# Attention scores from split queries and keys: one float32r product over 64 rows, and a second product for the maxima

## The chip, the cores and the metric

The kernel runs on one core of a Trainium2 chip. The metric is the device time of one execution in microseconds, the median of repeated runs. The core has a matrix engine (PE, with its weight loads PEld), three vector-like engines (DVE, ACT, POOL), SyncE (SP), whose queue issues every DMA of this kernel, and 16 DMA engines that share the transfers.

## The reference

A decoder layer on 32 samples of 256 tokens and 256 channels, with layer normalization after each of three blocks: a selective-scan block, cross attention with 16 heads of 16 channels, and eight gated experts, each for 32 of the 256 tokens of a sample.

```python
def reference(x, ctx, ...):
    x = layernorm(x + scan_block(x))            # xr = x W_in; conv; silu; dA, dBu; 4 chunks of 64 steps
    x = layernorm(x + cross_attention(x, ctx))
    x = layernorm(x + experts(x))               # silu(x w1) * (x w3), then w2

def cross_attention(query, ctx):                # 16 heads, d_k = 16
    q, k, v = proj(query, w_q, b_q), proj(ctx, w_k, b_k), proj(ctx, w_v, b_v)
    scores = einsum('bhqd,bhkd->bhqk', q, k) / sqrt(16)
    out = einsum('bhqk,bhkd->bhqd', softmax(scores), v)
    return einsum('bsd,ed->bse', merge_heads(out), w_o) + b_o
```

## The kernel before

**Order of the work.** The kernel is written as some 24 chains (Python generators, listed from L1255 on). Each chain yields the time at which its next step may begin and the engine of that step; `in_order` (L80) picks the earliest, with lags as tie breakers, and lets it emit its instructions. `spend` (L54) adds a planned cost to an engine's clock; the costs are constants in the text (`MM` 0.47 us a matmul, `GP` for POOL, `ISSUE` 0.62 and `LANDING` 3.5 for a DMA). The result is one fixed program order for each engine, SP included. At run time semaphores hold each engine at the head of its own order.

**Scan.** A sample has 16 steps of 32 channels. For a step, two loads (`load_step`, L519) copy delta and delta times u from DRAM (`dd`) into 128 partitions, eight copies of each channel pair; their source is [16, 8, 512] with a repeat in the middle. Loads are issued three steps ahead. ACT makes four exponentials (L573), DVE a product (L602) and the scan (L621), POOL multiplies by C (L637), PE sums (L651) and frees the six `h` buffers.

**Attention.** `keys_ahead` (L691) projects keys and values of a sample and stores them to DRAM (`k_all`, `v_all`); `queries` (L789) projects the queries from the normalized first block and stores them to `heads`. `spread_heads` (L678) loads both back so that 16 heads lie in 8 groups of two: head h is group h // 2, and its 16 channels begin at partition 64 (h % 2). `kT` and `qT` have 64 rows for each of two heads, of which rows 16 to 62 stay zero. A sample is worked in two halves of 8 heads, each loaded on its own; sample b's half waits until `attns` has scored that half of sample b - 1.

`maxima` (L825) computes the scores of two heads at a time, queries as weights, over 63 rows; DVE takes the row maxima (L838), PE transposes them, ACT negates them (L847), and two DMAs carry them through DRAM (`tops`) into row 63 of `qT`. Row 63 of `kT` is one (L272 to L275). `attns` (L874) then computes the scores again with keys as weights over all 64 rows, so that each score arrives with its row's maximum subtracted; ACT exponentiates (L894) and PE multiplies by the values (L863). `finish` (L924) normalizes, applies `w_o` and stores to `x2d`.

**Experts.** 32 units work on 256 tokens of one expert from eight samples, or, for the last eight samples, 128 tokens of each of two experts from four. A unit's tokens are read from `x2d` by `rows_of` (L1065), a block of [4, 32, 256] for each of two transfers, and results are stored in the same form to `out`. They fill PE time at low rank; the last four units can only begin when the last sample is stored.

**Shared parts.** Five PSUM banks go round through `take` and `done`. `heads(n)` (L166) loads the projection weights and biases for q and k, from an array padded to 32 columns for each head; these loads are put off into `later` and issued by `rest` (L363). `product` (L343) and `biased` (L352) are the helpers for a projection and its evacuation.

Of the kernel before, what the change touches and what calls it, by code (L numbers as in the profile page):

```python
# [7 lines left out]

F32 = mybir.dt.float32
AF = mybir.ActivationFunctionType  # L10
ALU = mybir.AluOpType
AX = mybir.AxisListType
# [3 lines left out]
P = 128  # L16
B, L, D = 32, 256, 256
# [14 lines left out]
H, DK = 16, 16  # L32
NG = 4
HG, HR = 8, 64
# [5 lines left out]
LANDING = 3.5  # L40
# [5 lines left out]
class Clock:  # L46
# [7 lines left out]
    def spend(self, engine, us, after=0.0):  # L54

        self.at[engine] = max(self.at[engine], after, self.base) + us
        return self.at[engine] + 0.3
# [40 lines left out]
def decoder_kernel(ctx: ExitStack, tc: tile.TileContext, a: dict, out: bass.AP):  # L98
    nc = tc.nc
    clock = Clock()  # L100
    spend = clock.spend

    def dma(dst, src):

        nc.sync.dma_start(dst, src)
        spend("SP", ISSUE)
# [4 lines left out]
    ident = cpool.tile([P, P], F32, name="ident")  # L111
# [3 lines left out]

    x2d = dram.tile([B, L, D], F32, name="x2d")

    k_all = dram.tile([B, D, L], F32, name="k_all")
    v_all = dram.tile([B, L, D], F32, name="v_all")

    ph = ctx
# [41 lines left out]
        dma(t, a[name].partition_broadcast(P))  # L163
        return t

    def heads(n):  # L166

        w = wp.tile([P, 2, D], F32, tag="w_" + n, name="w_" + n)
        src = a["w_" + n].rearrange("(k p) (h c) -> p k h c", p=P, c=32)
        for k in range(2):  # L170
            dst = w[:, k].rearrange("p (h c) -> p h c", c=DK)
            dma(dst, src[:, k, :, :DK])
        bias = wp.tile([P, 2], F32, name="b_" + n)
        for g in range(NG):
            r = 64 * (g % 2)
            src = a["b_" + n].rearrange("(j c) g -> j c g", c=32)[:, :DK, g : g + 1]
            dma(bias[r : r + 64, g // 2 : g // 2 + 1], src)
        return w, bias


# [25 lines left out]
            dma(at, src[j, g].unsqueeze(1).to_broadcast([DL, NL, NDC * NS]))  # L206
    nc.scalar.preload_act_table_set("natural_log_exp_and_others")

    later = []
    now, dma = dma, lambda dst, src: later.append((dst, src))  # L210
    w_k, b_k = heads("k")
    w_v = weight("w_v", D, D)
    b_out = row("b_out")
    w_out = weight("w_out", DI, D)
    w_q, b_q = heads("q")
    w_o = weight("w_o", D, D)
    b_o = row("b_o")
    b_v = wp.tile([P, 2, 1], F32, name="b_v")
# [49 lines left out]
    nc.gpsimd.memset(v[:, :, :, DK : DK + 1], 1.0)  # L268


    kT = keep.tile([P, HG, L], F32, name="kT")
    last = small.tile([P, 1], F32, tag="ln_st", name="last")  # L272
    at = ident.rearrange("p (j c) -> p j c", c=HR)[:, :, HR - 1]
    nc.vector.tensor_reduce(last, at, AX.X, ALU.add)
    nc.vector.tensor_copy(kT.rearrange("p g t -> p (g t)"), last.to_broadcast([P, HG * L]))  # L275
    qT = keep.tile([P, HG, L], F32, name="qT")
    nc.gpsimd.memset(qT, 0.0)

    tops = [keep.tile([P, 2, 4, 2], F32, name=f"tops_{i}") for i in range(2)]

# [82 lines left out]

    def rest():

        while later:
            yield 0.0, "SP"
            dma(*later.pop(0))

    xps, dds, sress, bcds, ygs, us, spread, silus = {}, {}, {}, {}, {}, {}, {}, []  # L370
    gated, stored = {}, []
# [303 lines left out]
    kts, qts, tts, vts, x1Ts, attended, oSs, ending = {}, {}, {}, {}, {}, [], [], []  # L675
    scored = {}

    def spread_heads(b, dst, d, t, there):  # L678

        yield t, "SP"  # L680
        for half in range(2):
            if b:
                yield lambda: max(t, scored[b - 1, half]) if (b - 1, half) in scored else None, "SP"
            for j in range(2):
                src = d.rearrange("(i g j c) t -> i j c g t", i=2, j=2, c=DK)[half, j]
                dma(dst[HR * j : HR * j + DK, 4 * half : 4 * half + 4, :], src)
            there[b, half] = clock.at["SP"] + LANDING

    made = []
# [1 line left out]
    def keys_ahead():  # L691

        for b in range(B):
            rank = lambda: 2 if b < len(begun) + 1 else 3
            yield lambda: None if later else spread.get(0), "SP"
            load_ctx(b)
            t0 = clock.at["SP"] + 2 * LANDING
            ctxT = cts.pop(b)
            yield from take(1, rank, t0)
            ps, t = product(  # L700
                "ps_qk",
                lambda j: [w_k[:, k, j * P : (j + 1) * P] for k in range(2)],
                lambda j: [ctxT[:, k, :] for k in range(2)],
            )
            yield t, "ACT"
            flat = unit1.tile([P, 2, L], F32, tag="k_flat", name=f"k_flat_{b}")
            tk = biased(flat, AF.Identity, b_k, ps, 0)
            done(1, tk)
            yield tk, "SP"
            dma(k_all[b].rearrange("(m p) t -> p m t", p=P), flat)  # L710
            yield from take(1, rank, t0)
            ps, t = product(
                "ps_v",
                lambda t: [ctxT[:, k, t * P : (t + 1) * P] for k in range(2)],
                lambda t: [w_v[:, k, :] for k in range(2)],
            )
            yield max(t, clock.at["SP"] + LANDING), "ACT"
            flat = unit1.tile([P, 2, D], F32, tag="k_flat", name=f"v_flat_{b}")
            nc.scalar.copy(flat, ps)
            t = spend("ACT", EV[2])  # L720
            done(1, t)
            yield t, "SP"
            dma(v_all[b].rearrange("(t p) c -> p t c", p=P), flat)
            made.append(clock.at["SP"] + LANDING)
# [64 lines left out]
    def queries():  # L789
        for b in range(B):  # L790
            yield lambda: x1Ts[b][1] if b in x1Ts else None, "PE"
            x1T, tx = x1Ts[b]
            yield from take(1, 2, tx)
            ps, t = product(
                "ps_qk",
                lambda j: [w_q[:, k, j * P : (j + 1) * P] for k in range(2)],
                lambda j: [x1T[:, k, :] for k in range(2)],
            )
            yield t, "ACT"
            del x1Ts[b]  # L800
            flat = unit1.tile([P, 2, L], F32, tag="q_flat", name=f"q_flat_{b}")
            tq = biased(flat, AF.Identity, b_q, ps, 0)
            done(1, tq)
            yield tq, "SP"
            d = bcd.tile([D, L], F32, tag="heads", name="heads")
            dma(d.rearrange("(m p) t -> p m t", p=P), flat)
            yield from spread_heads(b, qT, d, clock.at["SP"] + LANDING, qts)

    def scores(heads, left, right, n):


        ss = [bank("s").rearrange("p (t n) -> p t n", t=2) for _ in heads]
        for t in range(2):
            for h, s in zip(heads, ss):
                g, r = h // 2, HR * (h % 2)
                nc.tensor.matmul(  # L816
                    s[:, t, :],
                    left[r : r + n, g, t * P : (t + 1) * P],
                    right[r : r + n, g, :],
                    start=True,  # L820
                    stop=True,
                )
        return ss, spend("PE", 2 * MM + 0.2)

    def maxima():  # L825

        for i in range(2 * B):
            b, half = i // 2, i % 2
            at = b, half
            yield lambda: max(qts[at], kts[at]) if at in qts and at in kts else None, "PE"  # L830
            top, t0 = tops[half], max(qts[at], kts[at])
            h = 0
            while h < 8:
                yield from take(2, 2, t0)
                ss, ts = scores(range(8 * half + h, 8 * half + h + 2), qT, kT, HR - 1)
                for s in ss:
                    yield ts, "DVE"
                    nc.vector.tensor_reduce(top[:, h % 2, h // 2, :], s, AX.X, ALU.max)  # L838
                    t = spend("DVE", VE[2])
                    done(1, t)  # L840
                    h += 1
            yield from take(1, 1, t)
            ps = bank("ps_m")[:H, :P]
            nc.tensor.transpose(ps, top.rearrange("p j g t -> p (j g t)"), ident)
            yield spend("PE", 0.2), "ACT"
            rows = unit2.tile([H, P], F32, tag="rows", name="rows")
            nc.scalar.activation(rows, ps, AF.Identity, scale=-1.0)  # L847
            t = spend("ACT", 0.35)
            done(1, t)
            yield t, "SP"  # L850
            d = bcd.tile([2, 4 * L], F32, tag="tops", name="tops")
            dma(d.rearrange("j (i n) -> (j i) n", n=P), rows)
            yield clock.at["SP"] + LANDING, "SP"
            dst = qT[HR - 1 :: HR, 4 * half : 4 * half + 4]
            dma(dst.rearrange("j g t -> j (g t)"), d)
            tts[b, half] = clock.at["SP"] + LANDING

    def attend(g, ess):
# [15 lines left out]
    def attns():  # L874

        for n in range(2 * B):
# [4 lines left out]
            for g in range(3):  # L881
                ess = []
                while g < 2 and len(ess) < 4:
                    yield from take(2, 2, tq)
                    h = 8 * half + 4 * g + len(ess)
                    ss, ts = scores(range(h, h + 2), kT, qT, HR)
                    if g and not ess:
                        yield lambda: vts.get(b), "PE"
                        yield from take(1, 3, max(te, vts[b]))
# [34 lines left out]
    def finish(b):  # L924
# [25 lines left out]
        yield from take(1, 3, t)  # L950
        ps, t = transposes(att.rearrange("p t h d -> p t (h d)"))
        yield t, "ACT"
        aT = unit1.tile([P, 2, L], F32, tag="aT", name=f"aT_{b}")
        nc.scalar.copy(aT, ps)
        t = spend("ACT", EV[2])
        done(1, t)
# [385 lines left out]
```

## Time and profile before

| | us |
|---|---|
| runs | 2745.47, 2744.92, 2738.03; median 2744.92 |
| the profiled execution | 2743.78 |
| its span, first to last instruction | 2742.0 |
| first L621 scan starts | 44 |
| last L621 scan ends | 2513 |
| PE busy on score products (two L816 rows) | 345.4 + 313.8 |
| DVE busy on scans L621, products L602, maxima L838 | 1168.9, 626.1, 325.2 |
| POOL busy on L637 | 1209.1 |
| DMA | 505.86 MB in 491,497 packets |

A line of the profile names the source line, the engine, the operation, the tiles it writes and reads, shapes and the number of instructions; after the bar stand the busy time of the group in us and the mean ns of one, then the engine's idle time before them and what ended it. One f32 product of the program appears as two PE records. A DMA shows the landing of its parts in the updates of its semaphore, which the trace holds with their times. "Samples" below are the 32 entries of the batch.

### The profile page before, as it was taken

The page shows a single profiled execution, that of the slowest core. Times are in us where ns is not written, and L with a number is a line of the kernel's source. Part 1 is how long each engine was busy: PE and PEld are TensorE (multiplying, and loading weights), DVE is VectorE, ACT ScalarE, POOL GpSimd, SP SyncE. Part 2 cuts the span into 40 slices and gives each one's busy share as a digit, 9 for nine tenths or more (in the row PEclk, how much of TensorE's full clock was granted, in tenths as well). Part 3 has the DMA queues.
Part 4 walks back from the last instruction along what each step waited for, and adds up shares of the span by engine and source line. Part 5 has one row for each costly group of instructions (what it writes and reads, how often), then busy time and mean ns, then how long its engine had stood idle before and what let it go on. Part 6 is the DMA issues. An engine that isn't in the chain of part 4 may idle for free.

```text
span 2742.0 us, 48659 instructions
## 1 busy us (share of the span) xinstructions
PE 2466.3 (90%) x16964; PEld 1705.3 (62%) x16964; DVE 2380.6 (87%) x2413; ACT 2043.4 (75%) x4327; POOL 1643.7 (60%) x1145
## 2 busy tenths in 40 slices
PE   5788989889899899989998989999999899998988
PEld 4565666566566666666666666665666566666767
DVE  4999999999999999999999999999999899896212
ACT  6887888888778878887878778888788788674331
POOL 4775766666666666575666665666666666553000
PEclk8899999999999999998999999999999999999999
DMA  7866666666676666676666666667666566666464
GB/s 203 228 199 176 193 187 181 189 191 191 187 199 186 181 167 190 176 197 177 167 198 187 198 175 186 187 177 195 190 197 179 163 172 180 185 174 181 150 195 144
DMA packets 491497, 505.86 MB, mean 184 GB/s; under 512 B 177204, under 2 KB 339252, under 8 KB 491252
## 3 DMA queue, kind: packets, MB, share of 16 engines
q1 hardware_dynamic: 491252, 502.75, 64.8%
q8 instruction: 135, 2.21, 0.4%
q14 instruction: 110, 0.90, 0.1%
HBM read 426.07 MB, written 76.55 MB: 183 GB/s over the span
## 4 chain that ended last, share of the span: by engine, by line
PE 29%; DVE 11%; ACT 8%; DMA 5%; issue 3%; POOL 1%; SPq 1%; DVEq 0%; ACTq 0%; POOLq 0%
PE ps_h L1133 8%; PE s L816 6%; DVE h L621 5%; PE ps_down L1212 4%; ACT da L573 3%; PE y L651 3%; DVE bu L602 2%; DVE tops L838 2%; PE ps_in L349 2%; PE ps_oT L863 2%; DMA ld<-dd 1%; DMA xe<-x2d 1%; PE ps_out L349 1%; PE ps_qk L349 1%; ACT es L894 1%
## 5 line engine op out<-in xcount | busy, mean ns | idle before, releaser
L637 POOL TENSOR_TENSOR h<-h,c_bc 128x1024 f32<-128x1024 f32 x512 | 1209.1, 2362 | 740.6 <-DVE h L621 627.0
L621 DVE TENSOR_TENSOR_SCAN h<-da,bu 128x1024 f32<-128x1024 f32 x512 | 1168.9, 2283 | 50.4 <-ACT da L573 5.8
L573 ACT ACTIVATE da<-ld,a_neg 128x252 f32<-128x252 f32 x2048 | 864.6, 504 | 188.3 <-DVE h L621 138.4
L602 DVE TENSOR_TENSOR bu<-ld,b_bc 128x1024 f32<-128x1024 f32 x512 | 626.1, 1223 | 19.9 <-DMA ld<-dd 8.0
L816 PE MATMUL s<-kT,qT 63*128 63x256 f32 x2048 | 345.4, 416 | 45.6 <-DVE tops L838 22.8
L894 ACT ACTIVATE es<-s 128x512 f32<-128x512 f32 x512 | 277.9, 594 | 140.6 <-PE s L816 75.9
L838 DVE TENSOR_REDUCE tops<-s 128x2 f32<-128x512 f32 x512 | 325.2, 677 | 41.6 <-PE s L816 41.1
L1133 PE MATMUL ps_h<-x2T,w 128*128 128x256 f32 (+2 forms) x1536 | 343.5, 368 | 9.5 <-ACT es L894 1.7
L816 PE MATMUL s<-qT,kT 64*128 64x256 f32 x2048 | 313.8, 405 | 22.5 <-DMA qT<-tops 13.0
L651 PE MATMUL y<-h,sel_y 128*32 128x256 f32 x4096 | 280.8, 397 | 52.3 <-POOL h L637 36.9
L816 PEld LDWEIGHTS s<-kT,qT 63*128 63x128 f32 x2048 | 213.8, 193 | 151.9 <-DVE tops L838 50.8
L1133 PEld LDWEIGHTS ps_h<-x2T,w 128*128 128x128 f32 (+1 forms) x1536 | 246.7, 186 | 89.7 <-issue 35.1
L349 PE MATMUL ps_in<-xT,w_in 128*128 128x256 f32 x1024 | 258.4, 397 | 8.7 <-ACT da L573 2.6
L816 PEld LDWEIGHTS s<-qT,kT 64*128 64x128 f32 x2048 | 200.9, 189 | 102.3 <-issue 39.6
L651 PEld LDWEIGHTS y<-h,sel_y 128*32 128x32 f32 x4096 | 131.8, 113 | 177.4 <-POOL h L637 55.1
L349 PEld LDWEIGHTS ps_in<-xT,w_in 128*128 128x128 f32 x1024 | 192.8, 196 | 60.4 <-issue 12.9
L420 POOL TENSOR_TENSOR u<-u,shifted 128x512 f32<-128x512 f32 x128 | 151.4, 1183 | 39.7 <-ACT u L407 34.7
L323 POOL TENSOR_SCALAR ln_rstd<-ln_mv 128x2 f32<-128x2 f32 x96 | 20.9, 218 | 254.2 <-DVE ln_mv L320 250.0
L407 ACT ACTIVATE shifted<-ps_in,tap_b,conv_w 128x256 f32<-128x256 f32 x256 | 130.8, 567 | 22.5 <-PE ps_in L349 10.9
L863 PE MATMUL ps_oT<-es,v 128*32 128x256 f32 x2048 | 142.4, 391 | 3.7 <-DVE h L1197 1.2
L349 PE MATMUL ps_out<-w_out,yg 128*128 128x256 f32 x512 | 117.6, 383 | 0.4 <-DVE yg L667 0.4
L375 ACT ACT_TABLE_LOAD x90 | 115.5, 1283 | 1.4
(135 smaller groups left out, 2987.5 us busy)
## 6 DMA issues: line engine op xcount, KB each, us to landing
ld<-dd SPq DMA_DIRECT2D x1024, 256.0 KB
w<-in_w SPq DMA_DIRECT2D x128, 352.0 KB
x<-in_x SPq DMA_DIRECT2D x64, 256.0 KB
dd<-delta SPq DMA_DIRECT2D x32, 512.0 KB
dd<-u SPq DMA_DIRECT2D x32, 512.0 KB
w<-in_w SPq DMA_DIRECT2D x32, 384.0 KB
w13y<-in_w SPq DMA_DIRECT2D x32, 352.0 KB
c_bc<-bcd SPq DMA_DIRECT2D x64, 128.0 KB
```

Source lines behind the costliest of these rows:

```text
L349: nc.tensor.matmul(ps[:, j, :], l, r, start=(k == 0), stop=(k == len(terms) - 1))
L420: nc.gpsimd.tensor_tensor(u[:, cc], u[:, cc], at, ALU.add)
L573: nc.scalar.activation(da[:, g, q].rearrange("p (k t) -> p k t", t=CHUNK)[:, :, 1:], loads[i][:, 0, g].rearrange("p (k t) -> p k t", t=CHU ...
L602: nc.vector.tensor_tensor(bu, loads[i][:, 1].unsqueeze(2).to_broadcast([P, GB, NQ, L]), b_bc.unsqueeze(1).to_broadcast([P, GB, NQ, L]), AL ...
L621: nc.vector.tensor_tensor_scan(h.rearrange("p g q t -> p (g q t)"), das_of.pop(i).rearrange("p g q t -> p (g q t)"), bu.rearrange("p g q t ...
L637: nc.gpsimd.tensor_tensor(hs[i], hs[i], c_bc, ALU.mult)
L651: nc.tensor.matmul(y[32 * j : 32 * j + 32, :], sel_y[:, g, :], hs[i - NJ + 1 + j][:, g, q, :], start=(g == 0 and q == 0), stop=(g == GB - ...
L816: nc.tensor.matmul(s[:, t, :], left[r : r + n, g, t * P : (t + 1) * P], right[r : r + n, g, :], start=True, stop=True,)
L838: nc.vector.tensor_reduce(top[:, h % 2, h // 2, :], s, AX.X, ALU.max)
L863: nc.tensor.matmul(oT[32 * j : 32 * j + 32, :], v[:, k, 4 * g + j, :], ess[j][:, k, :], start=(k == 0), stop=(k == 1), tile_position=(0, 3 ...
L894: nc.scalar.activation(es, s, AF.Exp, scale=1.0 / DK**0.5)
L1133: nc.tensor.matmul(ps[:m, i, :], w_tiles[u, which, e][k][:, f * P : f * P + m], right, start=(k == 0), stop=(k == 1),)
```

## The change

The projections of keys and queries are split on POOL into a high part, rounded to float32r, and the remainder, also float32r (`parts_of`). Both parts are stored to DRAM, and loaded so that the 64 rows of a head hold, for keys, high, low, high, low, and for queries, high, high, low, low. One float32r product over the 64 rows then gives all four partial products. The row of maxima leaves `qT`; the negated maxima are split in the same way, into a tile `mT`, and a second product into the same bank, with a column of ones and zeros (`pick`) repeated as weights, adds them. Weights and biases of the two projections are put into another channel order, channel before head, so that a transfer's piece is 4 KB (four heads of 256 tokens) where it was 1 KB. The planned cost of a call of `scores` is lowered.

```diff
-    k_all = dram.tile([B, D, L], F32, name="k_all")
+    k_all = dram.tile([B, 2, 2, P, L], F32, name="k_all")
...
-    def heads(n):
+    def heads(n, tag):
...
+        raw = unit1.tile([P, 2, D], F32, tag=tag, name="raw_" + n)
...
+        def ordered():
+            for k in range(2):
+                for i in range(2):
+                    at = slice(i * P, (i + 1) * P)
+                    nc.gpsimd.tensor_copy(
+                        w[:, k, at].rearrange("p (j c g) -> p g j c", j=2, c=DK),
+                        raw[:, k, at].rearrange("p (g j c) -> p g j c", j=2, c=DK),
+                    )
+            spend("POOL", 1.6)
...
-    kT = keep.tile([P, HG, L], F32, name="kT")
...
-    qT = keep.tile([P, HG, L], F32, name="qT")
-    nc.gpsimd.memset(qT, 0.0)
+    kT = keep.tile([P, HG, L], F32R, name="kT")
+    qT = keep.tile([P, HG, L], F32R, name="qT")
+    mT = keep.tile([P, L], F32R, name="mT")
+    nc.gpsimd.memset(mT.bitcast(F32), 0.0)
+    pick = keep.tile([P, HG], F32R, name="pick")
...
-        while later:
+        while len(later) > 1:
             yield 0.0, "SP"
             dma(*later.pop(0))
+        yield clock.at["SP"] + 2 * LANDING, "POOL"
+        while orders:
+            orders.pop(0)()
+        dma(*later.pop(0))
...
+    def parts_of(n, b, full, t, d):
+
+        hi = unit1.tile([P, 2, L], F32R, tag="hi", name=f"{n}_hi_{b}")
+        lo = unit1.tile([P, 2, L], F32R, tag="lo", name=f"{n}_lo_{b}")
+        yield t, "POOL"
+        nc.gpsimd.tensor_copy(hi, full)
+        nc.gpsimd.tensor_tensor(lo, full, hi.bitcast(F32), ALU.subtract)
+        t = spend("POOL", 2 * GP[2])
+        yield t, "SP"
+        for s, part in enumerate((hi, lo)):
+            dma(d[:, s].rearrange("i p t -> p i t"), part.bitcast(F32))
...
             for j in range(2):
-                src = d.rearrange("(i g j c) t -> i j c g t", i=2, j=2, c=DK)[half, j]
-                dma(dst[HR * j : HR * j + DK, 4 * half : 4 * half + 4, :], src)
+                src = d[half, :, HR * j : HR * (j + 1), :].rearrange("s (c g) t -> s c (g t)", g=NG)
+                for s in range(2):
+                    r = HR * j + 2 * DK * s
+                    at = dst[r : r + 2 * DK, NG * half : NG * (half + 1), :]
+                    at = at.bitcast(F32).rearrange("p g t -> p (g t)")
+                    if dst is qT:
+                        dma(at, src[s].unsqueeze(0).to_broadcast([2, DK, NG * L]))
+                    else:
+                        dma(at, src)
...
-            yield tk, "SP"
-            dma(k_all[b].rearrange("(m p) t -> p m t", p=P), flat)
+            yield from parts_of("k", b, flat, tk, k_all[b])
...
-            yield tq, "SP"
-            d = bcd.tile([D, L], F32, tag="heads", name="heads")
-            dma(d.rearrange("(m p) t -> p m t", p=P), flat)
+            d = bcd.tile([2, 2, P, L], F32, tag="heads", name="heads")
+            yield from parts_of("q", b, flat, tq, d)
...
-                    left[r : r + n, g, t * P : (t + 1) * P],
-                    right[r : r + n, g, :],
+                    left[r : r + HR, g, t * P : (t + 1) * P],
+                    right[r : r + HR, g, :],
                     start=True,
-                    stop=True,
+                    stop=not lowered,
                 )
-        return ss, spend("PE", 2 * MM + 0.2)
+            for h, s in zip(heads, ss):
+                g, r = h // 2, HR * (h % 2)
+                if lowered:
+                    nc.tensor.matmul(
+                        s[:, t, :],
+                        pick[r : r + HR, g : g + 1].to_broadcast([HR, P]),
+                        mT[r : r + HR, :],
+                        start=False,
+                        stop=True,
+                    )
+        return ss, spend("PE", 0.7 if lowered else 0.4)
...
-            rows = unit2.tile([H, P], F32, tag="rows", name="rows")
+            rows = unit1.tile([H, P], F32, tag="rows", name="rows")
...
-            yield t, "SP"
-            d = bcd.tile([2, 4 * L], F32, tag="tops", name="tops")
-            dma(d.rearrange("j (i n) -> (j i) n", n=P), rows)
+            yield t, "POOL"
+            both = unit1.tile([H, 2, P], F32R, tag="both", name="both")
+            nc.gpsimd.tensor_copy(both[:, 0], rows)
+            nc.gpsimd.tensor_tensor(both[:, 1], rows, both[:, 0].bitcast(F32), ALU.subtract)
+            yield spend("POOL", 0.8), "SP"
+            d = bcd.tile([2, H, P], F32, tag="tops", name="tops")
+            dma(d.rearrange("s x n -> x s n"), both.bitcast(F32))
             yield clock.at["SP"] + LANDING, "SP"
-            dst = qT[HR - 1 :: HR, 4 * half : 4 * half + 4]
-            dma(dst.rearrange("j g t -> j (g t)"), d)
+            for j in range(2):
+                r = HR * j + 8 * half
+                src = d[:, 8 * j : 8 * j + 8, :].rearrange("s (g t) n -> s g (t n)", t=2)
+                dma(mT[r : r + 8].bitcast(F32), src)
...
-        aT = unit1.tile([P, 2, L], F32, tag="aT", name=f"aT_{b}")
+        aT = unit1.tile([P, 2, L], F32, tag="x1T", name=f"aT_{b}")
```

Smaller edits of the same change: `heads` issues eight bias loads where it issued four, and takes its `raw` tile from a buffer that the attention uses later.

## The prediction

> **What bounds the kernel now.** I read the busy times and slices first, then the window table, the groups of the touched lines, the chain of waits at the end, and last the DMA issues with the landings behind them.
>
> ```profile
> PE 2466.3 (90%) x16964; PEld 1705.3 (62%) x16964; DVE 2380.6 (87%) x2413; ACT 2043.4 (75%) x4327; POOL 1643.7 (60%) x1145
> ...
> DVE  4999999999999999999999999999999899896212
> ...
> q1 hardware_dynamic: 491252, 502.75, 64.8%
> ```
> ```profile
> 1439.55:1508.10 68.55, 61.68 (x422) 42.84 (x418) 66.84 (x63) 55.79 (x120) 46.03 (x30) 0.95 0.64 187
> ...
> 2536.35:2604.90 68.55, 63.79 (x470) 49.99 (x470) 20.46 (x41) 26.68 (x51) 3.61 (x9) 0.94 0.48 150
> ```
>
> The first columns of a window are PE, PEld, DVE, ACT and POOL busy, the last two DMA share and GB/s. Until about 2513 us, where the last L621 scan ends, DVE is busy 66.84 of 68.55 us; PE is close behind with 61.68. After that DVE falls to 20.46 and PE alone sets the pace with the expert units. The first scans of the samples start every 74.4 us from sample 2 (176 us) to 10 (771 us), and every 78.0 us from there to sample 29 (2254 us), when expert units run beside them. So there are two stages: 44 to 2513 us, where the DVE row and its feed decide, and 229 us of PE-bound tail.
>
> ```profile
> L816 PE MATMUL s<-kT,qT 63*128 63x256 f32 x2048 | 345.4, 416 | 45.6 <-DVE tops L838 22.8 <-DMA qT<-heads 5.9 <-ACT u L407 2.8
> ...
> L816 PE MATMUL s<-qT,kT 64*128 64x256 f32 x2048 | 313.8, 405 | 22.5 <-DMA qT<-tops 13.0 <-DVE tops L838 2.7 <-DVE yg L667 2.2
> ...
> L786 POOL TENSOR_TENSOR x<-x,b_o 128x512 f32<-128x512 f32 x32 | 40.7, 1271 | 9.9 <-PE ps_tr L340 9.9
> ```
> ```profile
> 2635.91 3.21 DMA x2d<-x
> 2640.97 9.79 DMA xe<-x2d
> ...
> 2664.03 7.88 DMA xe<-x2d
> ```
> ```profile
> ld<-dd SPq DMA_DIRECT2D x1024, 256.0 KB
> ...
> kT<-k_all SPq DMA_DIRECT2D x128, 64.0 KB
> ...
> qT<-heads SPq DMA_DIRECT2D x128, 64.0 KB
> ...
> xe<-x2d SPq DMA_DIRECT2D x64, 128.0 KB
> ```
>
> The second block is from the chain that ended last (start, us, what): a 256 KB store lands in 3.21 us, two 128 KB loads take 9.79 and 7.88. The reason is in the semaphore updates of the trace. A DMA raises its semaphore once for each engine that finishes its share: ld, kT, qT and x2d show 16 such landings, xe<-x2d and out<-xe five and qT<-tops three, of which one comes at 0.95 us, before any data, so four and two carry data. What these three share is the outermost dimension on one side: `rows_of` (L1065) gives [4, 32, 256] although SBUF has 128 partitions, qT<-tops has two rows. b_k, [4, 16, 1] into 64 partitions, shows five as well. The two xe loads of a unit are issued 0.59 us apart and land 2.06 us apart (median), which they would not do on different engines; two neighbouring kT loads land 0.29 us apart. An ld issued just behind such a pair lands after 6.25 us instead of 3.72: it queues behind them on those engines.
>
> **The change, part by part.**
>
> *Scores on PE.* A call of `scores` (2 heads, 2 tiles) is 8 records today, two per f32 matmul, and takes 1.06 to 1.14 us in the timeline; its 8 weight loads take 0.73. The trace holds no float32r product. Low bound: weight loads alone, 4 x 0.09 = 0.37 us for a maxima call and 0.73 for an attend call with its second product. High bound: one record per matmul at today's spacing, 0.57 and 1.13. Between: 0.47 and 0.93, so 256 x (1.10 - 0.47) + 256 x (1.10 - 0.93) = 205 us of PE freed, 6.4 us a sample. Were float32r as dear as f32, the second products would instead cost 256 x 1.1 = 282 us. In the main stage DVE's own work (66.84 of 68.55) lets only some 2 of the 78 us go: a base of 76 us.
>
> *Splits on POOL.* Two [128 x 512] operations for k and two for q: 4 x 1.27 (L786 row) = 5.1 us a sample, plus four on [16 x 128], bounded by 0.2 (L323 row, 218 ns) and 0.7, say 1 us. POOL goes from 46 to about 52 us of 68.55-us windows and stays under DVE; the work sits in time in which L637 waits for the scan (627 us in all). I cost it at 0; uncovered it is 6 x 32 = 190 us.
>
> *SP.* Twelve more issues a sample (four kT, four qT, two flat stores, two reads of tops) at about 0.42 us (median kT issue): 5 us of a queue that waits 668.7 us for DVE L602 alone; 0. The stores now wait for POOL where they waited for ACT; ld issues queue behind them, and that would show as DMA ld waits of L573 (44.4 us today). At the start eight more bias issues of 0.55 us, two reorderings and a wait of two landings delay `keys_ahead`, not the first scan: 0, else 12 us.
>
> *mT.* All 64 rows of a row group are read, so the write of half 1 and the attend calls of half 0 exclude each other. Today 13 of 32 samples issue the second tops read before the last attend call of half 0: 13 x 3.0 us (median landing) = 39 us of PE wait, inside what PE gains.
>
> *The new kT and qT loads.* Each was 64 KB with an outermost 16. Now a transfer is 32 rows of 4 KB, 128 KB, and its source is [2, 16, 1024]: for kT the two parts, for qT a repeat of one part. By the xe, out, b_k and tops rows, such a transfer runs on 2 engines, 16 packets of 4 KB on each. Packets of 4 KB took 159 ns at best (median), 182 in the w_in load at the start, 253 in the main stage. I take 182, because the other 14 engines will idle more. One transfer is then 2.9 us; a sample has 16: 46.6 us, always on the same two engines (41 to 65).
>
> What those engines carry already: 64.8% of 2742 us is 1777, or 55.5 us a sample. The xe and out loads, 128 transfers x 32 packets x 55 ns = 225 us, lie on four engines instead of their average 56: +5.3. The tail's traffic (229 us at 52%) goes off: -3.7. That is 57 us. Dropped 64 KB loads and added flat stores are both 16,384 packets of 1 KB, 1.8 us, and cancel. **57 + 46.6 = 104 us a sample against 78.** With every packet at its median (46 instead of 55 ns) it is 48 + 41 = 89; at 253 ns, 122.
>
> The same by the queue: ld is issued 8.4 us (median) before its exponential and lands in 3.9, so it stands 4.5 us of delay. A group of four transfers takes 11.7 us, its issues 1.7 of them: 5.4 us late. kT's two halves come alone, qT's together (23.3 - 4.5 - 3.4 = 15.4). 76 + 2 x 5.4 + 15.4 = 102. What is late next: ACT L573, then DVE L621 and POOL, and PE in `maxima`, behind whose wait for qT stand y and the expert units.
>
> A repeat of two as outermost dimension is not in the trace (repeats of 16 and 128, c_bc and b_out, show 16 landings). If it did not count, only kT would be narrow: 76 + 2 x 5.4 = 87.
>
> [...] The nearest rows, where only the outermost size told, also speak for 104, which I use.
>
> **Sum.** 44 us to the first scan, 64 for sample 0, 31 x 104 = 3224, and a tail of 229 (sample 31 pays some 35 us for its loads and gets as much back from PE): 3561 us of span. The profiled execution took 2743.78 for a span of 2742.0 and lies 1.1 us under the median of 2744.92, so 3563 as a time.
>
> **Rivals.**
> 1. *Narrow, but half hidden*: qT's repeat does not count, or the engines' queues fill the gaps. 44 + 64 + 31 x 87 + 229 = 3034. For it: no small repeat in the trace. Against: the budget of engine 0 alone asks 89 with both.
> 2. *The other side: faster.* The transfers spread over 16 engines after all; then 2 MB more a sample at 17.8 GB/s for each of 16 engines (505.86 MB in 64.8% of 2742 us) are 7 us beside a DMA share of 0.64, hidden. Main stage 19 x 2 = 38 us less, and freed PE time takes two to three expert units of 16 us out of the tail: 2742 - 38 - 45 = 2660. It decides if the two-part source shows 16 landings. Against it: four rows with a small outermost size, without exception.
> 3. *Spread, but held up by the splits*: flat stores wait for POOL at the head of SP, ld behind them. 2 x 2.5 us a sample, 160, against the 83 won: 2820.
>
> **How the numbers follow.** Forecast 0.79, rival 1 0.11, rival 2 0.06, rival 3 0.03, no change 0.01. The measurement tells 0.3% apart, 8 us. Faster 0.06, same 0.01, slower 0.93. The time is the forecast's. Its ends: 89 us a sample gives 44 + 64 + 2759 + 229 = 3096, 122 gives 4119; the price of 253 was taken among 16 busy engines and is less likely. I hold 3050 to 4000, which leaves part of rival 1 below.
>
> **What would show it.** kT<-k_all and qT<-heads as 256 transfers each of 128 KB, three landings each and 6 us or more to land; waits of ACT L573 for DMA ld grown from 44 us to several hundred; DMA share falling although bytes grow by 64 MB; DVE busy share down to 65 to 70%; sample starts about 104 us apart. Shorter L816 rows with PE busy near 2260 us would confirm the PE part, 1-us POOL rows the splits. Sixteen landings on kT would make the prediction wrong; three on kT and sixteen on qT would be rival 1; long SP waits for POOL rival 3.

## The result and the profile after

The changed kernel takes 3790.05 us (median of 3782.89 to 3794.09) against 2745.01: 1.3812 times the kernel before, 95% interval 1.3782 to 1.3843. The profiled execution's span is 3789.2 us.

Busy times, slices and the DMA queue of the changed kernel's page:

```profile
PE 2526.8 (67%) x15940; PEld 1735.4 (46%) x15940; DVE 2402.5 (63%) x2413; ACT 2043.6 (54%) x4329; POOL 1802.3 (48%) x1409
...
DVE  4766667666676665667666677666577666556321
...
PEclk8788778777888787888877787777768788778888
...
q1 hardware_dynamic: 507860, 570.90, 52.0%
```

DVE's busy time is that of before (2402.5 against 2380.6 us), only spread over 1047 us more. DMA moves 68 MB more and is busy a smaller share of the 16 engines: 52.0% where it was 64.8. An average over 16 engines does not show two that carry far more than the rest. The trace does not name a packet's engine, but an estimate can be made from its packet times: if the 4 KB packets of the scan stage (2879 us between 60 and 3538 us) lie on two engines, and every engine has a sixteenth of the other 26,072 us, then two engines are busy 88% of that stage and fourteen 47%. What was waited for shows more directly what that does. (The PEclk row, the granted clock in tenths, is lower than before almost throughout; the last section comes back to it.) From the view of waits (who waited, for whom; us in total, times, longest), first one line of the kernel before, then the engines of the changed kernel, then its SP queue:

```profile
ACT da L573 <- DMA ld<-dd: 44.4, 17, 6.0
```
```profile
ACT da L601 <- DMA ld<-dd: 942.0, 115, 26.3
...
DVE tops L892 <- PE s L860: 679.3, 109, 23.1
...
PE s L860 <- DMA qT<-heads: 410.7, 64, 16.0
```
```profile
SPq L106 <- DVE bu L630: 369.8, 156, 9.2
SPq L106 <- DMA qT<-heads: 183.0, 102, 3.9
SPq L106 <- DMA kT<-k_all: 161.0, 89, 3.8
```

ACT's wait for ld was 44.4 us and is now 942.0. The scan's loads are late, and so are the scores of the maxima, for qT. SP itself now waits 344 us for kT and qT to land, in many waits of up to 3.9 us; the same list of the kernel before has no line for either.

The issues and their sizes, and one stretch of SP's queue (start, us, what):

```profile
kT<-k_all SPq DMA_DIRECT2D x256, 128.0 KB
qT<-heads SPq DMA_DIRECT2D x256, 128.0 KB
```
```profile
1666.25 2.69 SPq L106 DMA_DIRECT2D kT<-k_all  x4
1668.99 5.45 SPq L106 DMA_DIRECT2D qT<-heads  x4
1674.55 3.33 SPq L106 DMA_DIRECT2D ld<-dd  x2
...
1684.30 19.60 SPq L106 DMA_DIRECT2D ld<-dd  x6
```

Six ld issues, 0.58 us each, spread over 19.6 us. The window table shows the stretch behind such a group (PE, PEld, DVE, ACT, POOL busy, granted clock, DMA share, GB/s), beside the one before it:

```profile
1600.00:1668.00 68.00, 57.23 (x331) 40.65 (x330) 53.68 (x58) 47.03 (x96) 38.38 (x34) 0.90 0.59 174
1668.00:1736.00 68.00, 35.48 (x226) 23.47 (x224) 34.02 (x40) 26.05 (x57) 20.36 (x15) 0.70 0.36 104
```

All compute engines lose a third to a half of their work at once, and the DMA share falls with them: what stops is the feed; no compute engine is full. The landings, read from the semaphore updates:

```
load, kernel            updates per transfer   us to land, median (90th percentile)
kT<-k_all  before       16                      3.65  (4.81)
kT<-k_all  after         3                     10.29 (14.42)
qT<-heads  before       16                      3.23  (4.62)
qT<-heads  after         3                     14.77 (19.16)
ld<-dd     before       16                      3.88  (5.80)
ld<-dd     after        16                      5.10 (12.84)

issue, us   transfer   semaphore   last landing, us
1799.22     qT         100         1808.41
1803.95     ld         108         1817.04
1808.43     ld         100         1817.70
1811.27     kT         101         1820.24      (semaphore 101 before: qT, landed 1811.20)
```

Of the three updates one comes at 1.05 us, before any data (the first 4 KB packet starts 1.37 us or more after the issue). The other two, for qT at 14.17 and 14.77 us, I read as those of two engines that carry data, and the packets agree: between 60 and 3538 us some 4 KB packet is in flight for 1449 us in all, for 1307 of them exactly two are, for 61 more than two. The lower list shows a second brake: the program uses eight DMA semaphores in turn, and an issue waits until the transfer that used its semaphore eight issues ago has landed. Here it starts 0.02 to 0.07 us after that landing. So behind a slow group SP cannot even issue the next loads.

### The profile page after: what moved, and what is told of

Read it like the earlier page. It is cut to its first block, busy times and chain, and to the rows that moved or that the text cites. A ratio compares the mean times of both kernels' runs of the same rounds, so it can differ in the third digit from the quotient of the medians.

```text
span 3789.2 us, 47464 instructions
## 1 busy us (share of the span) xinstructions
PE 2526.8 (67%) x15940; PEld 1735.4 (46%) x15940; DVE 2402.5 (63%) x2413; ACT 2043.6 (54%) x4329; POOL 1802.3 (48%) x1409
## 5 line engine op out<-in xcount | busy, mean ns | idle before, releaser
L601 ACT ACTIVATE da<-ld,a_neg 128x252 f32<-128x252 f32 x2048 | 863.9, 503 | 1039.1 <-DMA ld<-dd 942.0
L860 PE MATMUL s<-kT,qT 64*128 64x256 f32 x1024 | 198.1, 406 | 576.5 <-DMA qT<-heads 410.7
L860 PEld LDWEIGHTS s<-kT,qT 64*128 64x128 f32 x1024 | 123.2, 238 | 683.4 <-issue 576.8
L679 PE MATMUL y<-h,sel_y 128*32 128x256 f32 x4096 | 336.8, 448 | 110.3 <-POOL h L665 82.6
L1193 PE MATMUL ps_h<-x2T,w 128*128 128x256 f32 (+2 forms) x1536 | 374.5, 392 | 22.8 <-ACT da L601 8.8
L373 PE MATMUL ps_in<-xT,w_in 128*128 128x256 f32 x1024 | 294.1, 439 | 31.1 <-ACT v_flat L765 12.9
L870 PE MATMUL s<-mT,pick 64*128 64x256 f32 x1024 | 174.6, 315 | 100.0 <-DMA mT<-tops 99.9
L860 PE MATMUL s<-qT,kT 64*128 64x256 f32 x1024 | 201.7, 350 | 58.3 <-ACT es L954 23.6
L923 PE MATMUL ps_oT<-es,v 128*32 128x256 f32 x2048 | 171.1, 427 | 34.9 <-ACT es L954 30.3
L860 PEld LDWEIGHTS s<-qT,kT 64*128 64x128 f32 x1024 | 128.8, 207 | 137.0 <-issue 44.3
L870 PEld LDWEIGHTS s<-mT,pick 64*128 64x128 f32 x1024 | 129.8, 212 | 107.4 <-DMA mT<-tops 106.8
```

What stands on the lines that cost most here:

```text
L373: nc.tensor.matmul(ps[:, j, :], l, r, start=(k == 0), stop=(k == len(terms) - 1))
L601: nc.scalar.activation(da[:, g, q].rearrange("p (k t) -> p k t", t=CHUNK)[:, :, 1:], loads[i][:, 0, g].rearrange("p (k t) -> p k t", t=CHU ...
L679: nc.tensor.matmul(y[32 * j : 32 * j + 32, :], sel_y[:, g, :], hs[i - NJ + 1 + j][:, g, q, :], start=(g == 0 and q == 0), stop=(g == GB - ...
L860: nc.tensor.matmul(s[:, t, :], left[r : r + HR, g, t * P : (t + 1) * P], right[r : r + HR, g, :], start=True, stop=not lowered,)
L870: nc.tensor.matmul(s[:, t, :], pick[r : r + HR, g : g + 1].to_broadcast([HR, P]), mT[r : r + HR, :], start=False, stop=True,)
L923: nc.tensor.matmul(oT[32 * j : 32 * j + 32, :], v[:, k, 4 * g + j, :], ess[j][:, k, :], start=(k == 0), stop=(k == 1), tile_position=(0, 3 ...
```

## The experiments

Ratios are against the kernel before, run beside each on the same chip. A sample's time is the mean distance of the first scans of samples 2 to 31, 77.7 us before and 110.7 in the changed kernel.

**Outermost dimension 16.** The channels go first; number, size and 4 KB packets of the transfers stay.

```diff
-src = d[half, :, HR * j : HR * (j + 1), :].rearrange("s (c g) t -> s c (g t)", g=NG)
+src = d[half, :, HR * j : HR * (j + 1), :].rearrange("s (c g) t -> c s (g t)", g=NG)
...
-    dma(at, src[s].unsqueeze(0).to_broadcast([2, DK, NG * L]))
+    dma(at, src[:, s].unsqueeze(1).to_broadcast([DK, 2, NG * L]))
```

> The changed kernel with the dimensions of the kT and qT loads put in another order: same number, bytes and packets, but the source's outermost dimension is 16 channels instead of 2. Theory (two engines carry the loads): 16 landings per load, ACT's wait for DMA ld falls from 942 us to under 100, samples 76 us apart, 2600 to 2720 us. Rival (2 MB more a sample, the POOL splits, or a longer attention chain): little moves, over 3300 us.

2864.99 us, ratio 1.0434 (1.0401 to 1.0466): 925 of the 1045 us are gone. Each load shows 16 landings, in 4.01 and 3.96 us; a sample takes 81.6 us. From its page and its waits:

```profile
PE 2362.0 (83%) x15940; PEld 1631.9 (57%) x15940; DVE 2390.9 (84%) x2413; ACT 2047.5 (72%) x4329; POOL 1805.9 (63%) x1409
...
q1 hardware_dynamic: 515028, 570.93, 72.1%
```
```profile
ACT da L601 <- DMA ld<-dd: 123.0, 46, 7.7
```

The same bytes now keep 72.1% of the engines' time busy instead of 52.0, and the wait for ld falls from 942.0 to 123.0 us. That settles the cause of the 925 us. But the time is 145 us above the expected upper end, the wait is over the 100 us and the sample over the 76 us that I expected: with its kT and qT loads spread, the change is still slower than the kernel before, not faster. (The small mT<-tops loads, 8 KB each, still show three landings here, in 2.58 us, as qT<-tops did before; no run spreads them.)

**kT or qT alone on 16 engines.** A load of 32 rows is cut into two of 16, each with the outermost 16, for one of the two tensors. The second list is that with `if dst is qT`.

```diff
+if dst is kT:
+    for i in range(2):
+        put = dma if i else nc.sync.dma_start
+        put(at[DK * i : DK * (i + 1)], src[s if dst is qT else i])
-if dst is qT:
+elif dst is qT:
```

> Only the kT loads spread: each cut into two of 16 rows with outermost 16 (eight more issues a sample), qT as in the changed kernel. Theory: the two engines carry 57 + 23 us of qT, 80 to 90 us a sample, 2850 to 3150 us. Rival (bytes or chain): over 3300 us.

> Only the qT loads spread, kT as in the changed kernel, eight more issues a sample. Theory: as much engine time saved as with kT spread, 2850 to 3150 us; somewhat less than there if the burst of qT just ahead of the maxima is what hurts. Rival (bytes or chain): over 3300 us.

3375.29 and 3378.35 us (one run each), 97.6 and 97.7 us a sample. Both miss the range of the theory by some 225 us and lie over 3300, where I had put the rival. That rival, the bytes or the chain, cannot be the main reason, because e1_outer16 moves the same bytes through the same chain in 2865 us. What fails is my price for one narrow tensor: the sum of engine time, 57 + 23 = 80 us, asks for almost no loss. Measured above the 81.6 us of e1_outer16, narrow qT adds 16.0, narrow kT 16.1, both together 29.1. The tensors weigh the same, and the two parts nearly add. The narrow tensor's loads land in 10.2 us in both runs, and ACT waits 583 and 637 us for ld. So a narrow load delays the scan's loads before its engines are full: by that sum they are busy 80 of the 97.6 us. (The eight more issues a sample are in these numbers.)

**Outermost dimension 4.**

```diff
+src = d[half, :, HR * j : HR * (j + 1), :].rearrange(
+    "s (l h g) t -> s h l (g t)", h=4, g=NG
+)
+for s in range(2):
+    for i in range(2):
+        r = HR * j + 2 * DK * s + DK * i
...
+        dma(at, src[s if dst is qT else i])
```

> All kT and qT loads as 64 KB transfers of 16 rows with outermost 4 (channels in another order, 16 more issues a sample). Theory: five landings, four packets of 4 KB on each of four engines, 32 x 4 x 0.181 = 23 us a sample there, 57 + 23 = 80 and some gaps: 80 to 88 us a sample, 2850 to 3050 us. Rival (bytes, chain, or the issues on SP): over 3300 us.

3121.38 us (one run), 90.1 us a sample, five landings. Four engines lie between two and sixteen, as the theory asks, but the time is 71 us above its range and the sample 2 us; the 16 more issues a sample are in it, and no run separates them.

**What keeps e1_outer16 slow.** Four edits of it, each of one suspect:

```diff
# e5_mT_halves
-    mT = keep.tile([P, L], F32R, name="mT")
+    mTs = [keep.tile([P, L], F32R, name=f"mT_{i}") for i in range(2)]
...
-                        mT[r : r + HR, :],
+                        mTs[h // 8][r : r + HR, :],
# e6_old_plan
-        return ss, spend("PE", 0.7 if lowered else 0.4)
+        return ss, spend("PE", 2 * MM + 0.2)
# e7_half_loads
-                for s in range(2):
+                for s in range(1):
# e8_no_split
-        for s, part in enumerate((hi, lo)):
-            dma(d[:, s].rearrange("i p t -> p i t"), part.bitcast(F32))
+        for s in range(2):
+            dma(d[:, s].rearrange("i p t -> p i t"), full)
```

> e1_outer16 with one mT tile for each half, so that the write of one half's maxima no longer excludes the attend products of the other. If that exclusion is what keeps e1_outer16 (2865 us) above the kernel before, it falls by 30 us or more; if not, it stays within 15 us.

> e1_outer16 with the planned cost of a call of scores back at 2 * MM + 0.2 = 1.14 us (measured: 0.43 and 0.66). If the order laid out with the lower costs is what hurts, it falls by 30 us or more towards 2745; if the cause lies in the work itself, it stays within 20 us or gets slower.

> e1_outer16 with only the first 32 of each head's 64 rows loaded (half the kT and qT transfers and bytes, 8 fewer issues a sample; the low part of the queries is left out of the scores). If DMA volume and issues keep e1_outer16 slow (DMA share 0.72, 4 KB packets at 256 ns), it falls by 40 to 100 us and the wait of ACT for ld from 123 towards 44 us; if not, within 20 us.

> e1_outer16 without the two POOL operations of parts_of: the projection is stored twice as it is (the split is left out). Same transfers. If the splits on POOL, in front of the stores on SP, are what hurts, it falls by 40 to 100 us; by my costing at 0, it stays within 20 us.

```
run             median us   ratio (95% interval)        clock
e1_outer16      2864.99     1.0434 (1.0401 to 1.0466)   0.898
e5_mT_halves    2848.53     1.0381 (1.0345 to 1.0416)   0.906
e6_old_plan     2900.64     1.0582 (1.0550 to 1.0613)   0.886
e7_half_loads   2807.94     1.0238 (1.0214 to 1.0262)   0.898
e8_no_split     2887.30     1.0529 (1.0499 to 1.0560)   0.883
```

```profile
ACT da L603 <- DMA ld<-dd: 75.5, 26, 7.2
```

Only half the loads (e7) makes e1_outer16 faster by more than the intervals: 57 us less, 54 by the ratios, which also take out that the four ran on another chip. The wait for ld falls to 75.5 us. But of the 61 us between the two profiled executions only 32 lie ahead of the end of the last scan, where a sample now takes 80.6 us instead of 81.6. The tail shrinks by 28, from 225 to 197 us, because more of the expert units' work, 2064 of its 2816 PE records instead of 1876, was placed ahead of that end. So the volume and the issues of the loads, which e7 halves together, are worth some 30 us in the scan stage; the rest comes with the order of the work. The exclusion through `mT` is worth some 16 us, if anything: the intervals overlap. The splits on POOL cost nothing that can be seen; without them the kernel is 22 us slower, perhaps because its order differs too. With the old planned costs, which change nothing but the order, it is 36 us slower. So differences of 1% between such kernels can come from the order alone.

**The products by themselves.** e1_outer16 with float32 tiles, and the kernel before with float32r tiles and a lower planned cost of a call of `scores`, but nothing else of the change:

```diff
# e9_f32_scores, on e1_outer16 (kT, qT, mT and pick)
-    kT = keep.tile([P, HG, L], F32R, name="kT")
+    kT = keep.tile([P, HG, L], F32, name="kT")
# e11_before_f32r, on the kernel before (kT and qT)
-    kT = keep.tile([P, HG, L], F32, name="kT")
+    kT = keep.tile([P, HG, L], F32R, name="kT")
...
-        return ss, spend("PE", 2 * MM + 0.2)
+        return ss, spend("PE", 0.45)
```

> e1_outer16 with kT, qT, mT and pick in float32: the same loads, splits and order, the products as f32 again (both for an attend call). By my PE term, some 280 us more PE work than before and 480 more than e1_outer16: above 3000 us if PE time counts. If the PE time that float32r frees is given back as a lower granted clock (0.898 in e1_outer16, 0.959 before), the clock comes back to 0.95 or more and the time stays below 2950 us.

> The kernel before with kT and qT as float32r, loads, rows and maxima as they were, and 0.45 us planned for a call of scores: one float32r product in place of each f32 one (the low parts of queries, keys and maxima are left out). Only the PE work moves, about 512 x 0.65 = 330 us of it. By my forecast's PE term some 80 us faster, 2640 to 2700 us. If the freed PE time comes back as a lower clock, or DVE is all that counts, 2700 us or more.

e9_f32_scores: 3006.09 us, ratio 1.0947 (1.0924 to 1.0970), clock 0.956. e11_before_f32r: 2735.85 us, ratio 0.9974 (0.9958 to 0.9990), clock 0.907. e9 is over 3000 us as the first theory asks, and its clock is back as the second asks, though the second wanted a time under 2950: float32r is worth 141 us there, where I had put the PE work that it saves at 480 us. In e11, with the loads, rows and maxima as they were, float32r brings 5 us by the medians (15 between the two profiled executions) where I had some 80. Its page, its score products, and the group of y, an f32 product that was not touched, with rows of the kernel before ahead of them:

```profile
PEclk8899999999999999998999999999999999999999
```
```profile
L651 PE MATMUL y<-h,sel_y 128*32 128x256 f32 x4096 | 280.8, 397 | 52.3 <-POOL h L637 36.9 <-ACT es L894 7.6 <-ACT k_flat L355 3.7
```
```profile
PE 2280.7 (84%) x14916; PEld 1559.2 (57%) x14916; DVE 2383.3 (87%) x2413; ACT 2049.1 (75%) x4329; POOL 1646.7 (60%) x1145
...
PEclk7889898889999999999789999997799999998989
```
```profile
L652 PE MATMUL y<-h,sel_y 128*32 128x256 f32 x4096 | 311.6, 418 | 81.2 <-POOL h L638 59.1 <-DVE tops L839 7.3 <-ACT es L895 5.2
...
L817 PE MATMUL s<-kT,qT 63*128 63x256 f32 x1024 | 171.0, 359 | 94.7 <-DVE tops L839 58.1 <-DMA qT<-heads 16.4 <-ACT u L408 6.7
...
L817 PE MATMUL s<-qT,kT 64*128 64x256 f32 x1024 | 155.5, 353 | 47.3 <-DMA qT<-tops 20.5 <-DVE tops L839 8.4 <-ACT es L895 6.8
```

The two rows of score products fall by 333 us, from 345.4 + 313.8 to 171.0 + 155.5 (by 314 where overlapping records count once), as expected. All of PE's busy time falls by 186 us only, from 2466.3, because the products that were not touched got slower: the granted clock drops below nine tenths in more slices than before, and a y product takes 418 ns on average instead of 397. The window table of 800 to 2500 us, first the kernel before, then e11:

```profile
800.00:2500.00 1700.00, 1566.99 (x10793) 1061.61 (x10791) 1588.66 (x1624) 1332.19 (x2819) 1081.65 (x745) 0.97 0.65 183
```
```profile
800.00:2500.00 1700.00, 1451.29 (x9573) 974.44 (x9573) 1592.84 (x1634) 1342.70 (x2827) 1084.11 (x749) 0.92 0.65 185
```

PE is relieved of 116 us there and DVE gets through the same work in the same time, 1588.66 and 1592.84 us busy. The last scan even ends at 2535 us instead of 2513, and the tail shrinks from 229 to 192: more of the expert units' work was done ahead of the last scan's end, 2068 of its 2816 PE records instead of 1842. So part of the freed PE time was filled with that work. The lower planned cost also changed the order, as in e6; how much of the 22 us that the scan stage lost is due to it, no run separates.

**The same fault in the kernel before.** xe and out, the 4-engine rows from which the forecast was made, put on 16 engines:

```diff
     def rows_of(t, u, j):
...
-        return t[b : b + FOUR, CT * e : CT * (e + 1), :]
+        return t[b : b + FOUR, CT * e : CT * (e + 1), :].rearrange("b c d -> c b d")
```

> The kernel before with the 32 tokens ahead of the 4 samples in the xe loads and out stores of the expert units (outermost 32 instead of 4; nothing else moves). Theory of few engines: 16 landings, xe lands in about 4 us instead of 6.0, ld behind it is no longer late, and the time falls by 5 to 30 us, most of it in the tail. Rival (number of engines doesn't matter here): within 5 us.

> e10_before_xe and e11_before_f32r together (the low parts of queries, keys and maxima are left out). If the two gains add, 20 + 5 us under the kernel before: 2705 to 2725 us. If the lower clock of float32r eats what the faster xe loads bring, 2725 to 2745.

e10_before_xe: 2720.45 us, ratio 0.9904 (0.9882 to 0.9926). xe lands in 3.37 us instead of 6.01 with 16 landings, an ld just behind a pair in 3.41 instead of 6.25, and ACT's wait falls from 44.4 us:

```profile
ACT da L573 <- DMA ld<-dd: 30.7, 11, 7.3
```

e12_xe_f32r: 2714.45 us, ratio 0.9885 (0.9855 to 0.9914), the fastest kernel of this study and in the range that I expected if the two gains add. But its interval overlaps that of e10_before_xe, so float32r's share of it is not shown.

## Why the prediction was right, point by point

**Two engines carry the kT and qT loads: right.** Three landings on all 512, the repeat of 2 included; the four rows of the kernel before had five with an outermost 4 and three with a 2. Those rows spoke for 104 rather than 87, though none of them held a repeat of two. Packets of 4 KB took 181 ns on average in the main stage; I had taken 182, so 46 us a sample on the two engines holds. e1_outer16 shows the cause: the order of two dimensions, nothing else, is worth 925 us, and e4_outer4 with four engines lies between.

**104 us a sample: right in kind, 6% short.** 110.7 was measured. The two terms of the queue sum were 76 us of base and 26.3 of lateness. e1_outer16 puts the base at 81.6 and the lateness at 29.1. The lateness was nearly right though its picture was not whole: I let ld wait in the engines' queues alone, while SP also held back its issues through the eight semaphores. The base was the term most mis-sized, 5.6 of the 8.4 us between 102.3 and 110.7. That the other sum, 57 + 46.6 us of engine time, came to the same 104 was partly luck: the same sum gives 80 us for one narrow tensor, where e2 and e3 measured 97.6 and 97.7. The queue sum does better there, 15.4 us of lateness for qT against 16.0 measured, though only 10.8 for kT against 16.1. In the sum of the span, 3561 against 3789: the 31 samples from sample 1 to the end of the scans took 110.0 us each instead of 104 (+187), sample 0 took 80 instead of 64 (+16), the tail 251 instead of 229 (+22), and the first scan came 3 us later.

**"In the main stage ... lets only some 2 of the 78 us go: a base of 76": wrong.** The base went up. The calls themselves were sized fairly: in e1_outer16 the median one, up to the start of what follows it, takes 0.60 us for the maxima (the quickest quarter 0.43 or less) and 0.68 for an attend call, where I had 0.47 and 0.93. But the sign that was to confirm the PE part, PE busy near 2260 us, failed: it is 2526.8 in the changed kernel, more than before, because PE spent 1549 us at half rate. (DVE's busy share, 63%, also lies just under the 65 to 70% expected.) What failed further is that freed PE time would shorten the main stage. e11 shows it without the other parts of the change: 186 us less PE busy time, a scan stage 22 us longer, a tail 37 us shorter (45 expected), 5 us in total by the medians.

**Rival 2 (2660 if the loads spread): wrong in sign.** They were spread, and it took 2865. "7 us beside a DMA share of 0.64, hidden" is a step that fell: at 72.1% the 4 KB packets took 256 ns instead of 181, and with half the loads the scan stage is 32 us shorter (e7). The 38 us that freed PE time was to take off the main stage fell with the base. Rival 1's number, 87 us a sample with one narrow tensor, was 98 in both cases: my slack of 4.5 us for an ld did not hide a group, and below a full engine lateness already costs.

**POOL splits at 0: held.** 0.61 + 1.27 us a tensor, and 0.72 for the maxima, 5.2 us a sample; e8 shows no cost. **mT: 39 us of PE wait, hidden:** PE waits 99.9 us for mT in the changed kernel and 15.9 in e1_outer16; a tile for each half brings some 16 us, within overlapping intervals (e5). **SP at 0: doubtful.** An issue of kT takes 0.62 us instead of 0.42, and the 344 us of semaphore waits came on top; what SP costs by itself no run separates from the narrow loads.

**Still open.** e7_half_loads is 2.4% slower than before and e11 is not. Between them lie the double stores, the second product, the splits, two small mT loads where one qT load was, and another order; no run parts them. That PE time can still count shows in e9_f32_scores: the work of e1_outer16 with f32 products keeps PE busy 90% of the span and takes 141 us more.

## What to carry to other kernels

Count a transfer's engines before its bytes: here the outermost dimensions set the number, and loads of 128 KB with an outermost 2 made the scan wait 942 us for its own loads while the mean DMA share fell to 52%. Put a dimension of 16 or 32 outermost on both sides (both were tried here, and these loads showed 16 landings); the order of rows inside a tile is often free. Before work is taken off an engine, look whether that engine ends the waits of the stage: in e11, PE at 92% beside DVE at 93% gave the scan stage nothing back.

## What the runs showed of the hardware that was not expected

Part of the freed PE time came back as a lower granted clock (0.907 in e11_before_f32r, 0.959 in the kernel before). The clock records show two rates only, full and half; at half rate PE spent 226 us in the kernel before, 507 in e11_before_f32r, 588 in e1_outer16, 1549 in the changed kernel, and 268 in e9_f32_scores, which does e1's work with f32 products. The short half-rate stretches last 3.4 us or multiples of it (6.8, 10.2, 13.7). Where the time at half rate is longer, the gaps in PE's work add up to more: stretches of over 1 us without a matmul come to 199 us before, 379 in e1 and 1162 in the changed kernel. The traces of the kernel before, e1, e9, e11 and the changed kernel say more. Cut each trace into windows of 3.41 us, on whose borders the rate changes, and take those at full rate. When PE was busy for less than 30% of a window, the next one ran at half rate in 179 of 179 cases; at 30 to 50% in 137 of 166; at 50 to 80% in 72 of 545; at 90% and more in none of 2335. So drops followed also on windows in which PE was busy for 30 to 50%, in the f32 kernels as in the others. Between 50 and 80%, the windows before a drop were filled with score products to 36%, the others to 17%; whether such products count for less is open. That the gaps cause the drops is my reading; no run filled them to test it.

float32r products of 64 rows by 256 columns take 0.43 us for four, from the first start to the start of what follows, where f32 takes 1.06 (medians over the calls of e11 for the attend products, and of the kernel before).

Narrow transfers queued behind one another: the loads of a qT group, issued 0.66 us apart, landed 2.55 us apart (medians of the changed kernel), about the 2.6 us that 16 packets of 4 KB take in a row (162 ns each, median). With two packets in flight, that is what the same two engines for all of them would give. By their landings the kT, qT and xe loads ran on 2, 4 and 16 engines in these runs, for an outermost 2, 4, and 16 or 32. Which engines these are, the "engine 0" of rival 1 among them, no run here shows.
